# Attention with a depthwise convolution: raw value weights kept apart, three bias rows together, and a later count

## The chip, the cores and the metric

The kernel runs on one core of a Trainium2 chip. A core has five engines with an instruction stream each: TensorE (PE, matrix products; PEld is its loading of the stationary operand), VectorE (DVE), ScalarE (ACT), GpSimd (POOL) and SyncE (SP, which here issues most of the DMAs). Matrix products read SBUF and write to PSUM, the accumulator memory[...]. The metric is the device time in microseconds (us) of one execution; less is better.

## The reference

Four images of 384 channels and 48 x 48 pixels. The queries get the layer-normalized result of a 7 x 7 depthwise convolution added.

```python
x_flat = x.reshape(B, C, N).transpose(0, 2, 1)
local = depthwise_conv_7x7(x, conv_w)          # then batch norm with given statistics
x_norm = _layernorm(x_flat, ln_gamma, ln_beta)
qkv = x_norm @ qkv_w.T + qkv_b
q, k, v = qkv[0], qkv[1], qkv[2]               # 8 heads of 48
q = q + _layernorm(local_flat, ln_gamma, ln_beta)
attn = softmax(q @ k.T * scale)
out = (attn @ v) @ proj_w.T + proj_b
out = x_flat + out
```

All is float32. `ln_gamma` is folded into the weights (each weight row times `gain`), and `ln_beta` into biases: `beta` times the raw weights gives one row of 384 numbers each for queries (0), keys (1) and values (2).

## The kernel before

A tile is eight image rows, that is 384 pixels, of all channels in three chunks of 128; an image has six such groups, and there are 24 tiles. Keys and values of an image stay in SBUF; the tiles of queries then pass one after the other.

The order of the work is written out by hand for TensorE, VectorE and ScalarE: each takes its instructions in the order in which the program text emits them. SP and POOL follow the same rule for the first loads.

**Loads.** The first group of x, then the slab for its convolution, then the three weight blocks of `qkv_wT` (values, keys, queries), then the groups 1 to 5 of x, then `w_o`. Values go straight into `w_v`; keys and queries into `staged[1]` and `staged[0]`, which lie in buffers that later hold keys.

**The start.** `warm` runs filler matmuls. `Norm` holds the steps of a layer norm: mean (L386 for a sum over one chunk, `mean_of` by L473), `centre` (L401), `squares` (L364), `root` (L406 to L408 on ScalarE), `newton` (L413, L414) and `scale` (L468). The convolution is a stream of VectorE operations, one for each tap and chunk, 147 a tile (L251 for the first tap of a chunk, L255 for the others); `convolve_first(n)` takes the next n. For the first tile, ten taps of chunk 0 are made on TensorE instead, by diagonal matrices (`make_diagonals` L263 on ScalarE, `first_products` L274), and added at L827. `AHEAD` is how many taps VectorE does ahead of the first root.

**Biases.** `shift_rows` (L569) multiplies `beta` with the raw weights: values first, in place before `scale_values` (L607) scales them, and keys and queries later. `rows_out` copies the rows to SBUF, `columns` (L596) turns them into columns with 1-row matmuls, and `key_bias`, `query_bias` add them. `scale_rows` (L614, L615) makes the scaled query and key weights.

**The groups of the first image.** `from_x(0, g)` makes three value blocks, three key blocks and three query blocks of group g, two at a time; each pair is one `next` for the products (L473) and one for the ScalarE copies (L506, L512, L525). `both` takes both steps. Between them VectorE normalizes group g + 1, and in the last group the first convolved tile. Pairs use the PSUM buffers of `two_banks`, which alternates between two pools of two buffers.

**The attention.** `attend` makes scores (L767), exponentials on ScalarE (L775) and weighted sums (L788). Twelve slots of two halves make a tile; `plan` shares out the convolution of the coming tiles over the half slots, from the number of taps already done, an estimate of VectorE's spare time (`room`) and the slot by which a tile has to be convolved (`due`). ScalarE's squares for the coming norm (L369) are taken between the exponentials, and wait for VectorE's centring (L445).

**The tail.** Six groups of output projections (L473, L743 adds the residual, L746 sends them out). `divide` gives the reciprocals of the last softmax sums; L1039 multiplies the last outputs by them. `judge[0]` (L1059, L1061) counts sums outside a safe range, `judge[1]` makes a flag of the count, `judge[2]` reads it to decide on a second pass, which does not run here.

Of the kernel before, what the change touches and what calls it, by code (L numbers as in the profile page):

```python
# [10 lines left out]
F32 = mybir.dt.float32  # L11
# [4 lines left out]
P = 128  # L16
# [10 lines left out]
X_LATER = 3  # L27
OUT_SLOT = 4
LAG = 2
AHEAD = 9  # L30
WARM = 12
PE_TAPS = 10

# [5 lines left out]
def segments(a: bass.AP):  # L39

    heads = a[0:288].rearrange("(c h d) f -> h d c f", c=3, h=2)
    tails = a[288:384].rearrange("(h c r) f -> h r c f", h=2, c=3)
    return [(0, heads[0]), (48, tails[0]), (64, heads[1]), (112, tails[1])]
# [3 lines left out]
def unshifted_pass(  # L47
# [16 lines left out]
    nc = tc.nc  # L64
    B, C, N = x.shape
    W = 48
    H = N // W
    CC = C // P
    G = RG * W
    NG = N // G  # L70
# [5 lines left out]
    NT = B * NG  # L76
# [3 lines left out]
    big = ctx.enter_context(tc.tile_pool(name="big", bufs=1))  # L80
    work = ctx.enter_context(tc.tile_pool(name="work", bufs=2))
# [15 lines left out]
    def two_banks():  # L97
        return next(either)()
# [38 lines left out]
    cw, shift, gain, beta = vec[:, :, 0:T0], vec[:, :, T0], vec[:, :, T0 + 1], vec[:, :, T0 + 2]  # L137
# [31 lines left out]
    for c in range(CC):  # L169
        for r, n, first in ((0, HD, 0), (64, HD, 1), (48, 16, 6), (112, 16, 7)):  # L170
            head = first + 2 * c if first < 6 else first
            ch = head * HD + (16 * c if first >= 6 else 0)
            while n:
# [5 lines left out]
                r, n, ch = r + part, n - part, ch + part  # L179
# [4 lines left out]
    w_v = const.tile([P, CC, C], F32, tag="w_v", name="w_v")  # L184
# [2 lines left out]
        work.tile([P, 2, C], F32, tag="pt", name="pt", bufs=5) for _ in range(-(-PE_TAPS // 6))  # L187
    ]
    staged = [
        big.tile([P, CC, C], F32, tag=f"k{NG - 1 - i}", name=f"staged{i}") for i in range(2)  # L190
    ]
    load_packed(w_v, qkv_wT[:, 2 * C :])
    load_packed(staged[1], qkv_wT[:, C : 2 * C])
    load_packed(staged[0], qkv_wT[:, 0:C])
    for g in range(1, NG):
# [1 line left out]
    with nc.allow_non_contiguous_dma(reason="a few vectors, once"):  # L197
        for j in range(2):
            r = 64 * j
# [30 lines left out]
    def conv_ops(t):  # L230
# [10 lines left out]
        if t == 0:  # L241
            mine = [(tap, 0) for tap in taps[PE_TAPS:]]
            order = mine[:AHEAD] + [o for o in order if o[1]] + mine[AHEAD:]
        for tap, c in order:
# [23 lines left out]
    def first_products(n):  # L268

        slab, first, end = slabs[0, 0]  # L270
        for _ in range(n):
            i, tap = coming_products.popleft()
            src, part = window(slab, first_sum, 0, first, end, 0, tap)
            nc.tensor.matmul(  # L274
                part, lhsT=diagonal(i), rhs=src, start=i == 0, stop=i == PE_TAPS - 1
            )
# [45 lines left out]
    each = CC * KS * KS  # L322
# [226 lines left out]
    def both(making):  # L549
        next(making)  # L550
        next(making)
# [3 lines left out]

    row = work.tile([P, CC, G], F32, tag="rb", name="row", bufs=1)

    def of_row(i):  # L560
        return slice(64, 65) if i == 1 else slice(0, 1)

    rows = {}

    def shift_rows(some):
        r = two_banks()
        for c in range(CC):
            for i in some:
                nc.tensor.matmul(  # L569
                    r[of_row(i), i % 2, :C],  # L570
                    lhsT=beta[:, c : c + 1],
                    rhs=staged[i][:, c, :] if i < 2 else w_v[:, c, :],
                    start=c == 0,
                    stop=c == CC - 1,
                )
        rows.update((i, r[of_row(i), i % 2, :C]) for i in some)

    def rows_out(some):
        for i in some:
            dst = row[of_row(i), i].rearrange("o (u h d) -> o u h d", u=CC, h=2)  # L580
            nc.scalar.copy(
                dst[:, :, :, 0:HD], rows[i][:, 0:288].rearrange("o (u h d) -> o u h d", h=2, d=HD)
            )
            nc.scalar.copy(
                dst[:, :, :, HD:64],
                rows[i][:, 288:384].rearrange("o (h u r) -> o u h r", h=2, r=16),
            )

    def columns():

        r = two_banks()
        m = {}
        for i in range(CC):
            m[i] = r[:, i % 2, CC * i : CC * i + CC]
            for c in range(CC):
                nc.tensor.matmul(  # L596
                    m[i][:, c : c + 1],
                    lhsT=row[of_row(i), i, c * P : (c + 1) * P],
                    rhs=one[of_row(i)],
                    start=True,  # L600
                    stop=True,
                )
        return m

    def scale_values():
        for c in range(CC):
            nc.scalar.mul(w_v[:, c], w_v[:, c], gain[:, c : c + 1])  # L607

    def scale_rows(i, c):
        heads = staged[i][:, c, 0:288].rearrange("p (u h d) -> p u h d", h=2, d=HD)  # L610
        tails = staged[i][:, c, 288:384].rearrange("p (h u r) -> p h u r", h=2, r=16)
        for h in range(2):
            w = w_qk[:, c, i, :, 64 * h : 64 * h + 64]
            nc.scalar.mul(w[:, :, 0:HD], heads[:, :, h, :], gain[:, c : c + 1])  # L614
            nc.scalar.mul(w[:, :, HD:64], tails[:, h, :, :], gain[:, c : c + 1])  # L615

    def key_bias(m):
        nc.vector.tensor_add(qkb[:, 1, :], qk_vec[:, 1, :], m[1])
        nc.vector.tensor_add(vbp[:, :, 0], vbp[:, :, 0], m[2])

    def query_bias(m):

        nc.vector.tensor_add(qkb[:, 0, :], qk_vec[:, 0, :], m[0])
        nc.vector.tensor_add(qkb[:, 0, :], qkb[:, 0, :], beta)
# [192 lines left out]
    n_first = 0  # L817

    def convolve_first(n):
        nonlocal n_first  # L820
        n_first += n
        for _ in range(n):
            next(stream)

    def add_products():
        a = accs[0][:, 0, :]
        nc.vector.scalar_tensor_tensor(a, first_sum, shift[:, 0:1], a, ALU.add, ALU.add)  # L827
# [7 lines left out]
    norm = Norm(xn[0, 0])  # L835
# [4 lines left out]
    make_diagonals(0, 5)  # L840
    convolve_first(AHEAD)
    norm.mean_of(norm.buf)
    norm.root()
    make_diagonals(5, PE_TAPS)
    first_products(2)
    shift_rows((2,))
    scale_values()
    first_products(2)
    norm.scale(norm.newton())
    for c in range(CC):  # L850
        scale_rows(1, c)
    for g in range(NG):

        last = g == NG - 1
        making = from_x(0, g)
        both(making)
        if g == 0:
            first_products(PE_TAPS - 4)
        convolve_first(3 if g else 8)
        norm = Norm(accs[0] if last else xn[0, g + 1])  # L860
        norm.sum()
        norm.mean()
        if g == 0:
            shift_rows((1, 0))
            rows_out((2, 1, 0))
        convolve_first(6)
        norm.centre()
        norm.squares()
        next(making)
        if g == 0:  # L870
            add_products()
            m = columns()
            key_bias(m)
            query_bias(m)
        next(making)
        if g == 0:
            for c in range(CC):
                scale_rows(0, c)
        convolve_first(3)
        norm.sum_squares()  # L880
        norm.mean()
        norm.root()
        both(making)
        convolve_first(8 if last else 12)
        if last:
            local_end(0, norm.newton())
        else:
            norm.scale(norm.newton())
        both(making)
        both(making)  # L890
# [3 lines left out]
    for t in range(NT):  # L894
        b, g = divmod(t, NG)
        if g == 0 and b:
# [6 lines left out]
            for gk in range(NG):  # L903
                before = t - NG + gk
                load_residual(before)
                making = from_x(b, gk, before, ao if gk < NG - 1 else outputs[before][0])
# [12 lines left out]
                if gk == 1:  # L919
                    query_end(t)  # L920
                    rb = divide(t - 1)
# [25 lines left out]
        for s in range(NSLOT):  # L947
# [4 lines left out]
            if s == 2 and g:  # L952
                rb = divide(t - 1)
# [57 lines left out]
            if following and s == first - 1:  # L1011
                norm = Norm(accs[t + 1])
# [10 lines left out]
    pair_add()  # L1023
    for before in range(NT - NG, NT):
        ao = aos[before % NG]
        if before == NT - NG + 1:
            judge[0](two_banks()[:, 0, :])
        r, r2 = two_banks(), two_banks()
        parts = r[:, 0, :G], r[:, 1, :G], r2[:, 0, :G]
        for co, m in enumerate(parts):  # L1030
            project(m, lambda c: w_o[:, c, co * P : (co + 1) * P], lambda c: ao[:, c, :])
        for co, m in enumerate(parts):
            finish(before, co, m, nc.scalar)
        if before == NT - NG:
            rb = divide(NT - 1)
        if before == NT - NG + 1:
            judge[1]()
        if before == NT - NG + 2:
            nc.vector.tensor_mul(outputs[NT - 1][0], outputs[NT - 1][0], rb)  # L1039
        if before == NT - 2:  # L1040
            n_outside = judge[2]()
# [536 lines left out]
```

## Time and profile before

| what | value |
|---|---|
| median of three runs | 2867.02 us (2865.14 to 2868.14) |
| profiled execution: device time, span | 2866.66 us, 2864.8 us |
| TensorE busy | 2841.4 us, 99% |
| VectorE busy | 2341.4 us, 82% |
| ScalarE busy | 1650.2 us, 58% |
| mean granted TensorE clock | 0.997 |
| first score (L767) | at 150.94 us |
| last projection (L473) starts | at 2856.93 us |

The page sums up one execution. A line of groups gives the source line, engine, operation, tiles and shapes, then busy time and the mean of one; what stands after it in brackets or behind a bar is the idle time of the engine just before and the instruction that ended it. Matrix products in float32 are two instructions each in the trace, so a projection of three chunks is x6. A busy TensorE is not the same as a fast one: the granted clock is read from the stretches.

### The profile page before, as it was taken

Reading aid. Unit: us, or ns where it says so; the run is one execution under the profiler, and the core shown is the slowest. Engines: PE = TensorE matmul, PEld = TensorE weight load, DVE = VectorE, ACT = ScalarE, POOL = GpSimd, SP = SyncE. Lnnn points to the kernel's source line nnn. Section 1 sums busy time; section 2 is a strip of 40 time slices with the busy share of each in tenths; the row PEclk is TensorE's granted clock in tenths of the full one; section 3 lists DMA queues with packets and bytes.
Section 4 is the critical chain, followed back from the end, with each engine's and each line's share of the span. In section 5 each row is a group of like instructions: output and inputs, shape, how many; then the busy total and the mean of one; then the engine's idle time right before and its main releaser. Section 6 shows DMA issues by size and latency. Waiting matters only on the chain.

```text
span 2864.8 us, 70286 instructions
## 1 busy us (share of the span) xinstructions
PE 2841.4 (99%) x29540; PEld 1463.1 (51%) x29540; DVE 2341.4 (82%) x4613; ACT 1650.2 (58%) x2341; POOL 17.3 (1%) x82
## 2 busy tenths in 40 slices
PE   8999999999999999999999999999999999999998
PEld 5544455444554455555555445545555545555554
DVE  6999999999888988878888889887788887787301
ACT  4356666666226666666622666666652466666662
POOL 2000000000000000000000000000000000000000
PEclk9999999999999999999999999999999999999999
DMA  6101121111220211121132112102113111111111
GB/s 115 39 5 37 44 50 35 30 32 43 72 80 25 48 35 41 31 38 24 38 94 70 28 30 51 35 22 45 38 32 93 45 21 28 43 31 32 46 29 63
DMA packets 103688, 124.38 MB, mean 43 GB/s; under 512 B 43344, under 2 KB 89024, under 8 KB 103360
## 3 DMA queue, kind: packets, MB, share of 16 engines
q1 hardware_dynamic: 99568, 116.07, 17.0%
q8 instruction: 234, 3.83, 0.6%
q10 hardware_dynamic: 3088, 3.65, 0.4%
q14 instruction: 94, 0.77, 0.1%
q0 software_dynamic: 704, 0.06, 0.0%
HBM read 81.98 MB, written 27.03 MB: 38 GB/s over the span
## 4 chain that ended last, share of the span: by engine, by line
PE 95%; DVE 4%; DMA 1%; ACT 0%; issue 0%; SPq 0%; ACTq 0%; DVEq 0%
PE r L767 38%; PE o L788 38%; PE o L473 10%; PE r L473 9%; DVE acc L255 3%; ACT pt L775 0%; DMA xn<-in_x_dram 0%; DMA staged<-in_qkv_wT_dram 0%; DVE xn L401 0%; DMA vec<-natural 0%; PE o L386 0%; PE r L386 0%; DVE sq L375 0%; DMA taps_in<-in_conv_w_dram 0%; DVE sq L374 0%
## 5 line engine op out<-in xcount | busy, mean ns | idle before, releaser
L775 ACT ACTIVATE pt<-r 128x768 f32<-128x768 f32 x1728 | 1400.6, 811 | 754.6 <-PE r L767 738.6
L255 DVE SCALAR_TENSOR_TENSOR acc<-slab,vec,acc 128x368 f32<-128x368 f32 (+7 forms) x3447 | 1756.2, 582 | 3.9 <-DMA slab<-in_x_dram 2.7
L788 PE MATMUL o<-pt,v 64*64 64x384 f32 x13824 | 1440.9, 482 | 0.0
L767 PE MATMUL r<-xn,k 48*64 48x384 f32 x10368 | 1083.1, 482 | 4.8 <-ACT pt L775 4.8
L788 PEld LDWEIGHTS o<-pt,v 64*64 64x64 f32 x13824 | 555.9, 132 | 562.6 <-issue 540.3
L767 PEld LDWEIGHTS r<-xn,k 48*64 48x64 f32 x10368 | 418.9, 132 | 427.4 <-issue 370.5
L767 PE MATMUL r<-qt,kt 48*64 48x384 f32 x3456 | 358.8, 482 | 0.1
L767 PEld LDWEIGHTS r<-qt,kt 48*64 48x64 f32 x3456 | 135.6, 132 | 144.4 <-issue 134.6
L683 DVE TENSOR_TENSOR ao<-o,ao 113x384 f32<-113x384 f32 x72 | 39.9, 554 | 192.8 <-PE r L767 175.7
L473 PE MATMUL o<-xn,w_qk 128*128 128x384 f32 x438 | 149.3, 486 | 0.0
L473 PE MATMUL r<-xn,w_qk 128*128 128x384 f32 x426 | 147.2, 492 | 0.0
L473 PEld LDWEIGHTS o<-xn,w_qk 128*128 128x128 f32 x438 | 83.2, 190 | 58.0
L473 PEld LDWEIGHTS r<-xn,w_qk 128*128 128x128 f32 x426 | 82.1, 193 | 57.9 <-issue 2.7
L506 ACT COPY v<-r 128x384 f32<-128x384 f32 x44 | 19.0, 482 | 130.6 <-PE r L473 130.6
L473 PE MATMUL r<-w_v,xn 128*128 128x384 f32 x264 | 89.3, 487 | 1.2 <-DVE xn L468 1.2
L473 PE MATMUL o<-af,w_o 128*128 128x384 f32 x234 | 80.5, 495 | 0.0
L683 DVE TENSOR_TENSOR aot<-o,aot 113x384 f32<-113x384 f32 x24 | 13.3, 555 | 82.1 <-ACT aot L674 64.6
L374 DVE TENSOR_TENSOR sq<-sq 128x384 f32<-128x384 f32 x47 | 26.0, 554 | 56.2 <-ACT sq L369 56.2
L473 PEld LDWEIGHTS r<-w_v,xn 128*128 128x128 f32 x264 | 49.8, 190 | 37.5 <-issue 3.6
L473 PEld LDWEIGHTS o<-af,w_o 128*128 128x128 f32 x234 | 45.2, 193 | 31.7 <-issue 1.7
L473 PE MATMUL o<-w_v,xn 128*128 128x384 f32 x168 | 58.4, 487 | 0.1
L743 DVE SCALAR_TENSOR_TENSOR xr<-r,pb,xr 128x384 f32<-128x384 f32 x25 | 15.4, 618 | 48.6 <-ACT xn L525 41.7
(130 smaller groups left out, 1026.8 us busy)
## 6 DMA issues: line engine op xcount, KB each, us to landing
xr<-in_x_dram SPq DMA_DIRECT2D x24, 576.0 KB
slab<-in_x_dram SPq DMA_DIRECT2D x32, 378.0 KB
held<-ao SPq DMA_DIRECT2D x20, 576.0 KB
af<-held SPq DMA_DIRECT2D x20, 576.0 KB
xn<-in_x_dram SPq DMA_DIRECT2D x48, 216.0 KB
rb<-rden SPq DMA_DIRECT2D x48, 216.0 KB
out_dram<-xr SPq DMA_DIRECT2D x54, 192.0 KB
slab<-in_x_dram SPq DMA_DIRECT2D x16, 297.0 KB
```

The costliest lines, as they stand in the source:

```text
L255: nc.vector.scalar_tensor_tensor(dst, src, weight, dst, ALU.mult, ALU.add)
L374: nc.vector.tensor_add(self.buf[:, 0, :], src[:, 0, :], src[:, 1, :])
L473: nc.tensor.matmul(dst, lhsT=weights(c), rhs=src(c), start=c == 0, stop=c == CC - 1)
L506: nc.scalar.copy(v[:, blk, :, 0:HD], r[:, :C].rearrange("p (h d) -> p h d", d=HD))
L683: nc.vector.tensor_add(dst, sums[0 : 64 + HA, 1, :G], dst)
L743: nc.vector.scalar_tensor_tensor(xr[:, co, :], m, pb[:, co : co + 1], xr[:, co, :], ALU.add, ALU.add)
L767: nc.tensor.matmul(r[h, j, :G], lhsT=kk[:, blk * P + h.start : blk * P + h.stop], rhs=qq, start=True, stop=True,)
L775: nc.scalar.activation(pt, r[:, :, :G], AF.Exp, scale=SCALE)
L788: nc.tensor.matmul(sums[halves[j], i, :G], lhsT=values[t // NG, kb // NB][h, first : first + 64], rhs=pt[h, j, :], start=kb == 0, stop=kb ...
```

## The change

1. `AHEAD`: 9 taps ahead of the first root become 4.
2. The raw value weights are loaded into a third `staged` tile. `scale_values` reads it and writes `w_v`; it comes right behind the first root on ScalarE, ahead of the second half of the diagonals.
3. Of the ten products, five come before the first norm's scaling and five behind the rows (before: two, two, and six behind the first values).
4. All three rows are made at once behind the first two value blocks, at output partitions 0, 32 and 64 of one bank; `row` is one row long, and the columns use three banks in place of two.
5. Group 0 is written out apart: 14 taps behind the first values, the biases ahead of the third value and first key block (which come before centring), the query weights scaled behind the second root.
6. Groups 1 to 5 take 4 taps ahead of the sum in place of 3.
7. `judge[0]` and `judge[1]` move from the second to the fourth group of the tail.

```diff
-AHEAD = 9
+AHEAD = 4
...
-        big.tile([P, CC, C], F32, tag=f"k{NG - 1 - i}", name=f"staged{i}") for i in range(2)
+        big.tile([P, CC, C], F32, tag=f"k{NG - 1 - i}", name=f"staged{i}") for i in range(3)
...
-    load_packed(w_v, qkv_wT[:, 2 * C :])
+    load_packed(staged[2], qkv_wT[:, 2 * C :])
...
-    row = work.tile([P, CC, G], F32, tag="rb", name="row", bufs=1)
+    row = work.tile([P, CC, G], F32, tag="rb", name="row", bufs=1)[:, 0]
...
     def of_row(i):
-        return slice(64, 65) if i == 1 else slice(0, 1)
+        return slice(32 * i, 32 * i + 1)
...
         for c in range(CC):
-            for i in some:
+            for i in range(3):
                 nc.tensor.matmul(
-                    r[of_row(i), i % 2, :C],
+                    r[of_row(i), 0, :C],
                     lhsT=beta[:, c : c + 1],
-                    rhs=staged[i][:, c, :] if i < 2 else w_v[:, c, :],
+                    rhs=staged[i][:, c, :],
...
-        r = two_banks()
-        m = {}
-        for i in range(CC):
-            m[i] = r[:, i % 2, CC * i : CC * i + CC]
+        r, r2 = two_banks(), two_banks()
+        m = {1: r[:, 0, 0:CC], 2: r[:, 1, 0:CC], 0: r2[:, 0, 0:CC]}
+        for i in m:
...
-            nc.scalar.mul(w_v[:, c], w_v[:, c], gain[:, c : c + 1])
+            nc.scalar.mul(w_v[:, c], staged[2][:, c], gain[:, c : c + 1])
...
     norm.root()
+    scale_values()
+    first_products(5)
+    norm.scale(norm.newton())
     make_diagonals(5, PE_TAPS)
-    first_products(2)
-    shift_rows((2,))
-    scale_values()
-    first_products(2)
-    norm.scale(norm.newton())
     for c in range(CC):
         scale_rows(1, c)
-    for g in range(NG):
+
+    making = from_x(0, 0)
+    both(making)
+    shift_rows()
+    rows_out()
+    first_products(PE_TAPS - 5)
+    m = columns()
+    convolve_first(14)
+    norm = Norm(xn[0, 1])
+    norm.sum()
+    norm.mean()
+    add_products()
+    key_bias(m)
+    query_bias(m)
+    both(making)
+    convolve_first(3)
+    norm.centre()
+    norm.squares()
+    convolve_first(4)
+    norm.sum_squares()
+    norm.mean()
+    norm.root()
+    for c in range(CC):
+        scale_rows(0, c)
+    both(making)
+    convolve_first(10)
+    norm.scale(norm.newton())
+    both(making)
+    both(making)
+    for g in range(1, NG):
...
-        convolve_first(3 if g else 8)
+        convolve_first(4)
...
-        if before == NT - NG + 1:
+        if before == NT - NG + 3:
             judge[0](two_banks()[:, 0, :])
...
-        if before == NT - NG + 1:
+        if before == NT - NG + 3:
             judge[1]()
```

More of the change, by code (lines that the diff above doesn't have):

```diff
@@ L554, in unshifted_pass, with shift_rows @@
     qkb = const.tile([P, 2, CC], F32, tag="qkb", name="qkb")
-    row = work.tile([P, CC, G], F32, tag="rb", name="row", bufs=1)
+    row = work.tile([P, CC, G], F32, tag="rb", name="row", bufs=1)[:, 0]
+    rows = {}
     def of_row(i):
-        return slice(64, 65) if i == 1 else slice(0, 1)
-    rows = {}
-    def shift_rows(some):
+        return slice(32 * i, 32 * i + 1)
+    def shift_rows():
         r = two_banks()
         for c in range(CC):
-            for i in some:
+            for i in range(3):
                 nc.tensor.matmul(
-                    r[of_row(i), i % 2, :C],
+                    r[of_row(i), 0, :C],
                     lhsT=beta[:, c : c + 1],
-                    rhs=staged[i][:, c, :] if i < 2 else w_v[:, c, :],
+                    rhs=staged[i][:, c, :],
                     start=c == 0,
@@ L575, in shift_rows, with rows_out @@
                 )
[L576 to L580, printed above, removed]
+        rows.update((i, r[of_row(i), 0, :C]) for i in range(3))
+    def rows_out():
+        for i in (1, 2, 0):
+            dst = row[of_row(i)].rearrange("o (u h d) -> o u h d", u=CC, h=2)
             nc.scalar.copy(
@@ L597, in columns @@
                     m[i][:, c : c + 1],
-                    lhsT=row[of_row(i), i, c * P : (c + 1) * P],
+                    lhsT=row[of_row(i), c * P : (c + 1) * P],
                     rhs=one[of_row(i)],
@@ L856, in unshifted_pass @@
         both(making)
-        if g == 0:
-            first_products(PE_TAPS - 4)
-        convolve_first(3 if g else 8)
+        convolve_first(4)
+        assert not last or n_first >= each - PE_TAPS
         norm = Norm(accs[0] if last else xn[0, g + 1])
@@ L862, in unshifted_pass @@
         norm.mean()
-        if g == 0:
-            shift_rows((1, 0))
-            rows_out((2, 1, 0))
         convolve_first(6)
@@ L868, in unshifted_pass @@
         norm.squares()
[L869 to L878, printed above, removed]
+        both(making)
         convolve_first(3)
```

## The prediction

> **What bounds the kernel now.** First the page's busy shares and its chain of waits:
>
> ```profile
> PE 2841.4 (99%) x29540; PEld 1463.1 (51%) x29540; DVE 2341.4 (82%) x4613; ACT 1650.2 (58%) x2341; POOL 17.3 (1%) x82
> ...
> PE 95%; DVE 4%; DMA 1%; ACT 0%; issue 0%; SPq 0%; ACTq 0%; DVEq 0%
> ```
>
> TensorE sets the end, so only its idle time, its slow stretches, or work taken off it can be won. Next, who TensorE waited for over the whole span:
>
> ```profile
> PE r L767 <- ACT pt L775: 4.8, 8, 2.8
> PE o L386 <- DVE sq L375: 4.1, 2, 3.8
> PE r L1061 <- DVE outside L1059: 2.9, 1, 2.9
> PE o L832 <- POOL one L151: 1.9, 1, 1.9
> PE o L569 <- DMA w_v<-in_qkv_wT_dram: 1.8, 1, 1.8
> PE r L473 <- DVE xn L468: 1.2, 1, 1.2
> ```
>
> (columns: us in total, times, longest us.) Three places matter: the start (L386, L569, L473), one stall of 2.8 us among the scores (L767), and the count of the tail (L1061). The chain as a timeline of the start ends with these pieces:
>
> ```profile
> 41.01 0.57 DVE sq L375
> 41.58 0.14 issue
> 41.71 1.62 PE o L386 x2
> 43.33 6.00 PE r L473 x12
> 49.34 3.87 PE o L473 x12
> ```
>
> Up to 41.71 us TensorE is led by loads, VectorE and ScalarE; from there it is never idle for long until 311 us. Note 6.00 us for twelve matmul instructions that take 3.87 next time: the windows of 2 us show a granted clock of 0.67, 0.50, 0.50 and 0.62 from 40 to 48 us.
>
> **What the Trainium skill says.** (1) "TensorE: Matmul & The Clock Gate", Part 1, What's actually happening: after an idle window of some 3.4 us, in a grid that runs free of the kernel, the TensorE clock is halved until a window has been busy. The trace agrees: half clock after the idle stretch at 38 to 41.7 us and after the one at 2825 to 2828 us; the stall of 2.8 us at 311.9 us brought none, so the placing in the grid counts. (2) The same page, Part 3, Measured speedup vs the span model: three column tiles together give 2.38 times. The trace shows two: L569 with one row (x6) and with two rows (x12) each took 2.10 us. Three are not shown. (3) The same page, Architectural detail, on queues: ScalarE and VectorE take their instructions strictly in order. I use that for what stands behind what. No page gives a time for the loads of this start; the trace does.
>
> **The change, part by part.** I follow the new program order with old durations.
>
> *First root.* VectorE ran nine tap operations ahead of the first Newton step (L413), which had been ready on ScalarE's side much earlier:
>
> ```profile
> 13.81 5.47 DVE L255 SCALAR_TENSOR_TENSOR acc<-slab,vec,acc 128x329 f32<-128x329 f32 x9 [2.73 <-DMA slab<-in_x_dram]
> ...
> 15.41 0.52 ACT L408 ACTIVATE sq<-sq 128x384 f32<-128x384 f32 x1
> ...
> 19.20 0.61 DVE L413 SCALAR_TENSOR_TENSOR sq<-r,eps,sq 128x384 f32<-128x384 f32 x1
> ...
> 20.44 1.36 DVE L468 SCALAR_TENSOR_TENSOR xn<-xn,sq 128x1152 f32<-128x1152 f32 x1
> ...
> 21.94 4.11 PE L473 MATMUL r<-w_v,xn 128*128 128x384 f32 x12 [1.21 <-DVE xn L468]
> ```
>
> Four take 4 x 0.61 = 2.4 us, to 16.25, just past the root's end at 15.93. So the normalized group is there at 18.8 instead of 21.8, and the first values start at about 18.95: **3.0 us earlier**. Value weights: the load landed at 17.17 (L569 waited for it); scaling was in place behind that row, 18.03 to 19.93. Now it reads the raw copy, so starts at 17.2 and ends at 19.1; the third chunk is needed at 20.2, so it costs nothing. The five diagonals behind it (1.55) and the key rows (3.3) end at 23.9 on ScalarE, used only from 28 us. The SP queue issues the same loads in the same order, with another destination.
>
> *The rows.* First values end at 23.0. The three rows then need the query weights. Their landing is not shown; the neighbours landed at 17.17, 20.36 and, after it in the queue, 26.75 (first L374), some 3.2 us apart, so an estimate of 23.5; bounds 20.4 and 30.2, where the old rows ran without waiting. Cost of eighteen instructions: between 2.1 (three tiles together) and 4.2 us (a third alone). I take 2.1, to 25.7. Six ScalarE copies (0.54 per row) end at 27.4, hidden behind five products (10 x 0.32 = 3.2 us) to 28.85. The columns (1.49 as before) end at 30.3: before, 37.95.
>
> *The second normalization.* The 14 taps (7.1 us) end at 26.0, under the wait for the second group's load at 26.75; its sum ends at 28.0. The product addition at 28.9, four bias operations to 31.3, three taps to 32.9 and centring to 34.2. TensorE: mean, then third values and first keys to 34.85. Here order costs something: the squares (L364) now stand behind the ScalarE copies of these two, which wait for 34.85, so squares run 36.0 to 37.2; the four taps fit below. The sum of squares ends at 38.4 and the mean starts at 38.5 instead of 41.71: **3.2 us earlier**, after 3.65 us of idle (3.8 before).
>
> *What follows.* Mean and six key projections take 4.6 us at full clock. Query weights are scaled after the root, to about 45.1 on ScalarE, where they stood ahead of it before; at full clock the queries lose 0.5 to that. The group's last projection would then end at 49.4, against 55.0: 5.6 won. With the half clock as now it is 51.7: 3.3. The idle stretch is longer than the window, so I expect the half clock in most placings: **3.5 us**, ends 1.2 (rows not together) and 5.6.
>
> *Groups 1 to 5.* One more tap (0.55) ahead of each sum. VectorE's idle before L401 was 4.32, 1.77, 2.38, 0.86 and 0.49 us in turn, so it is hidden but for some 0.1 in the last. Total taps before the first scores: 154 becomes 156, that is 17 and 19 of the second tile.
>
> *The stall at 311 us.* VectorE is full from 160 to 313 us, and TensorE waits for it by way of ScalarE:
>
> ```profile
> 313.41 0.52 ACT L369 ACTIVATE sq<-acc 128x384 f32<-128x384 f32 x1 [3.83 <-DVE acc L445]
> ...
> 314.69 0.88 PE L767 MATMUL r<-xn,k 48*64 48x384 f32 x8 [2.80 <-ACT pt L775]
> ```
>
> Working out the planner's shares with 17 and with 19 gives the same running total, 302, at that slot. Two operations fewer are left: 2 x 0.52 = **1.0 us** off the stall (bounds 0 and 1.3).
>
> *The tail.* Now:
>
> ```profile
> 2827.91 0.21 PE L1061 MATMUL r<-outside,ones_col 128*1 128x24 f32 x2 [2.86 <-DVE outside L1059]
> 2828.04 1.26 PEld L473 LDWEIGHTS o<-af,w_o 128*128 128x128 f32 x5
> 2828.04 5.83 PE L473 MATMUL o<-af,w_o 128*128 128x384 f32 x12
> ...
> 2842.19 1.35 DVE L1039 TENSOR_TENSOR ao<-ao,rb 128x1152 f32<-128x1152 f32 x1
> ```
>
> Projections could have gone on at 2824.9: 3.15 us lost, and 1.8 more at half clock (5.83 against 4.03). Moved two groups on, the count is a new wait: it stands on VectorE behind the third addition of the group before (0.66 after the last matmul) and behind L1039 (1.35), then takes 0.18. Behind it on TensorE wait nine projections of the fourth group. Price about 2.6 us, with no gain of its own. The broadcast that L1039 needs was issued by 2830.4 and its traffic is over by about 2834, before 2837.3. The flag is read 5.8 us later; hidden. Net 4.95 - 2.6 = 2.35 at full clock, 0.65 with another half-clock window: **1.5 us**.
>
> Sum: 3.5 + 1.0 + 1.5 = **6.0 us**. The profiled span is 2864.8 (device time 2866.66), the median 2867.02: 2861.0.
>
> **The rivals.** *Full clock*: neither idle stretch falls on the grid: 5.6 + 1.0 + 2.35 = 9.0, so 2858. For it: the stall at 311.9; against it: 3.65 us exceed a window. *Gain mostly eaten*: the third column tile runs alone (2.1 us on TensorE's path) or the half clock lasts two windows: 1.2 + 1.0 + 0.65 = 2.9, so 2864.1. For it: two windows were lost at 40 us; against: two tiles already overlap fully. *Slower*: all three rows now wait for the last weight load, and products, columns and third values stand behind them. If it lands at the upper bound 30.2, TensorE idles 7 us from 23.0, everything behind moves by 6.6 and one half-clock window (1.7) follows: 3.5 - 8.3 + 2.5 = -2.3, so 2869.3, more with two windows. It decides from a landing some 6 us after my 23.5; loads landing 3.2 us apart in queue order speak against it.
>
> **How the numbers follow.** Forecast 0.50, with 2859 to 2863 as its own range; full clock 0.22; mostly eaten 0.20; slower 0.08. A measurement can tell about 0.2%, 5.7 us, so 2861.3 is a bound close to my figure: two thirds of the forecast's own chance lie beyond it (0.33), with full clock 0.55. Slower by that much: 0.06. Same: 0.39. The range 2856.5 to 2866 leaves out the slower case and the ends of the others.
>
> **What would show it.** First values near 19.0 us; L569 as eighteen instructions in 2.1 us near 23.6; L386 near 38.5; the first L767 near 147.5 instead of 150.94; the stall at L767 near 1.8; L1061 after L1039 with 2.5 us of idle. It is wrong if the rows wait past 25 us, if L386 is not earlier, or if a group after the first loses TensorE time to VectorE.

## The result

| | before | changed |
|---|---|---|
| median of 6 runs each, taken together | 2866.32 us (2865.14 to 2868.14) | 2858.84 us (2857.59 to 2860.61) |
| ratio | | 0.9973, 95% interval 0.9961 to 0.9986 |
| span of the profiled execution | 2864.8 us | 2857.1 us |

The change makes the kernel 7.5 us faster. The forecast was 6.0. In a second comparison (12 runs of the changed kernel) it was 2860.38 against 2866.35, that is 6.0 us, 0.9979 (0.9970 to 0.9987). The runs of the changed kernel differ among themselves by some 4 us; the experiments show one source, half clock that falls differently from one execution to the next.

Where the time went is read from fixed points of TensorE's work in the two traces (its timeline, start of an instruction):

| point | before | changed | ahead by |
|---|---|---|---|
| first values (L473) | 21.94 | 19.11 | 2.83 |
| mean of the second sum of squares (L386) | 41.71 | 37.78 | 3.93 |
| first values of group 1 | 54.98 | 49.87 | 5.11 |
| first score | 150.94 | 146.40 | 4.54 |
| end of the stall among the scores | 314.69 | 309.11 | 5.58 |
| first projection of the tail | 2818.97 | 2813.15 | 5.82 |
| last residual addition (VectorE) | 2859.07 | 2850.76 | 8.31 |
| end of the span | 2864.8 | 2857.1 | 7.7 |

So some 4.5 us come from the first image (5.1 from group 0, of which groups 1 to 5 lose 0.6), 1.0 from the stall, 0.2 from the long stretch behind it, and 2.5 from the tail, of which 0.6 are lost again behind the last addition.

The profile after, first who TensorE waited for over the whole span (us in total, times, longest):

```profile
PE o L386 <- DVE sq L375: 3.6, 2, 3.4
PE r L765 <- ACT pt L773: 3.4, 7, 1.8
PE r L1073 <- DVE outside L1071: 2.1, 1, 2.1
PE o L830 <- POOL one L151: 1.9, 1, 1.9
PE o L473 <- DVE xn L468: 1.7, 1, 1.7
PE o L386 <- ACT k L512: 1.1, 1, 1.1
```

The same three places remain: the wait for the second sum of squares (3.4 of it, 3.8 before), the stall of the scores (L765 is the old L767; 1.8, 2.8 before), and the count (L1073, the old L1061; 2.1, 2.9 before). New is the last line: 1.1 us behind a key copy in group 4.

The timeline of the start, with the first root, the first values, the three rows and the second mean:

```profile
14.01 2.44 DVE L255 SCALAR_TENSOR_TENSOR acc<-slab,vec,acc 128x329 f32<-128x329 f32 x4 [2.95 <-DMA slab<-in_x_dram]
...
16.36 0.61 DVE L413 SCALAR_TENSOR_TENSOR sq<-r,eps,sq 128x384 f32<-128x384 f32 x1
...
19.11 4.11 PE L473 MATMUL o<-w_v,xn 128*128 128x384 f32 x12 [1.72 <-DVE xn L468]
...
23.15 2.11 PE L568 MATMUL r<-staged,vec 128*1 128x384 f32 x18
...
34.44 0.48 ACT L506 COPY v<-r 128x384 f32<-128x384 f32 x1 [7.51 <-PE r L473]
34.81 0.59 ACT L512 ACTIVATE k<-r,qkb 128x384 f32<-128x384 f32 x1
35.29 1.16 ACT L364 ACTIVATE sq<-xn 128x1152 f32<-128x1152 f32 x1
...
37.78 0.88 PE L386 MATMUL o<-sq,mean_w 128*128 128x384 f32 x2 [3.38 <-DVE sq L375]
...
38.50 5.73 PE L473 MATMUL r<-xn,w_qk 128*128 128x384 f32 x12
```

All eighteen instructions of the rows (L568) take 2.11 us, as six did before. The squares stand on ScalarE behind the copies of the third values and first keys, as forecast; TensorE is idle for 3.38 us, and its next twelve matmul instructions take 5.73 us, not 4.03.

The tail, TensorE's and VectorE's timeline:

```profile
2831.41 1.35 DVE L1051 TENSOR_TENSOR ao<-ao,rb 128x1152 f32<-128x1152 f32 x1
2832.68 0.17 DVE L1071 TENSOR_SCALAR outside<-inside 128x24 f32<-128x24 f32 x1
...
2832.90 0.21 PE L1073 MATMUL r<-outside,ones_col 128*1 128x24 f32 x2 [2.06 <-DVE outside L1071]
...
2833.04 4.14 PE L473 MATMUL o<-af,w_o 128*128 128x384 f32 x12
```

The mark (L1071) waits behind the multiplication L1051, as forecast, and in this execution no half clock follows (4.14 us, 5.83 before).

### The profile page after: what moved, and what is told of

It is laid out like the page before. It is cut to its first block, busy times and chain, and to the rows that moved or that the text cites. A ratio compares the mean times of both kernels' runs of the same rounds, so it can differ in the third digit from the quotient of the medians.

```text
span 2857.1 us, 70279 instructions
## 1 busy us (share of the span) xinstructions
PE 2835.6 (99%) x29540; PEld 1447.8 (51%) x29540; DVE 2341.4 (82%) x4613; ACT 1650.3 (58%) x2341; POOL 17.3 (1%) x82
## 3 DMA queue, kind: packets, MB, share of 16 engines
q10 hardware_dynamic: 3088, 3.65, 0.4%
## 4 chain that ended last, share of the span: by engine, by line
PE 93%; DVE 5%; DMA 0%; ACT 0%; issue 0%; SPq 0%; DVEq 0%; ACTq 0%
PE r L765 37%; PE o L786 37%; PE o L473 10%; PE r L473 10%; DVE acc L255 4%; DMA slab<-in_x_dram 0%; ACT pt L773 0%; PE r L386 0%; PE o L386 0%; DVE sq L375 0%; PE o L274 0%; DVE sq L374 0%; DVE acc L401 0%; DVE xn L401 0%; DVE ao L681 0%
## 5 line engine op out<-in xcount | busy, mean ns | idle before, releaser
L255 DVE SCALAR_TENSOR_TENSOR acc<-slab,vec,acc 128x368 f32<-128x368 f32 (+6 forms) x3447 | 1756.5, 584 | 4.1 <-DMA slab<-in_x_dram 2.9
L765 PE MATMUL r<-xn,k 48*64 48x384 f32 x10368 | 1081.3, 482 | 3.4 <-ACT pt L773 3.4
L786 PEld LDWEIGHTS o<-pt,v 64*64 64x64 f32 x13824 | 549.9, 132 | 568.9 <-issue 541.4
L765 PEld LDWEIGHTS r<-xn,k 48*64 48x64 f32 x10368 | 414.7, 132 | 430.0 <-issue 370.4
L765 PE MATMUL r<-qt,kt 48*64 48x384 f32 x3456 | 357.7, 482 | 0.1
L765 PEld LDWEIGHTS r<-qt,kt 48*64 48x64 f32 x3456 | 133.4, 132 | 146.5 <-issue 135.0
L473 PE MATMUL r<-xn,w_qk 128*128 128x384 f32 x432 | 148.9, 490 | 0.0
L473 PE MATMUL o<-xn,w_qk 128*128 128x384 f32 x432 | 147.2, 486 | 0.0
L473 PEld LDWEIGHTS r<-xn,w_qk 128*128 128x128 f32 x432 | 82.8, 192 | 58.2 <-issue 1.8
L473 PEld LDWEIGHTS o<-xn,w_qk 128*128 128x128 f32 x432 | 82.1, 190 | 57.2
L473 PE MATMUL r<-w_v,xn 128*128 128x384 f32 x258 | 87.3, 487 | 0.0
L473 PE MATMUL o<-af,w_o 128*128 128x384 f32 x222 | 75.0, 486 | 0.0
L473 PEld LDWEIGHTS r<-w_v,xn 128*128 128x128 f32 x258 | 48.8, 190 | 35.2 <-issue 1.8
L473 PE MATMUL o<-w_v,xn 128*128 128x384 f32 x174 | 60.3, 486 | 1.7 <-DVE xn L468 1.7
L473 PEld LDWEIGHTS o<-af,w_o 128*128 128x128 f32 x222 | 42.1, 190 | 29.2
```

The lines of the kernel that those rows point to most:

```text
L255: nc.vector.scalar_tensor_tensor(dst, src, weight, dst, ALU.mult, ALU.add)
L473: nc.tensor.matmul(dst, lhsT=weights(c), rhs=src(c), start=c == 0, stop=c == CC - 1)
L765: nc.tensor.matmul(r[h, j, :G], lhsT=kk[:, blk * P + h.start : blk * P + h.stop], rhs=qq, start=True, stop=True,)
L786: nc.tensor.matmul(sums[halves[j], i, :G], lhsT=values[t // NG, kb // NB][h, first : first + 64], rhs=pt[h, j, :], start=kb == 0, stop=kb ...
```

## The experiments

My theory was the sum of the prediction: three places on TensorE's path, each with a local gain that is kept to the end. The first rival was that VectorE, which is full up to the stall, takes the start's gain back. The second was that the half clock, and with it mostly luck, makes the difference. Each kernel was compared with the kernel before in the same group of runs; "against before" is the difference of these medians. The changed kernel itself stands at 7.5 and 6.0 us faster by this measure. The intervals of most variants overlap with its own, so a difference of some 3 us from the changed kernel is not told by the totals alone; it is read from the traces, one execution of each kernel.

### The count of the tail put back (a1_count_back)

```diff
-        if before == NT - NG + 3:
+        if before == NT - NG + 1:
             judge[0](two_banks()[:, 0, :])
...
-        if before == NT - NG + 3:
+        if before == NT - NG + 1:
             judge[1]()
```

> The changed kernel with the count of the tail back in its second group. Sum of local gains (my theory): TensorE waits about 2.9 us for the mark of the sums again, where it waits 2.06 us now, and a window of half clock may follow (1.8 us); the other half of the change keeps its gain. 1.9 to 2.6 us slower than the changed kernel, about 2861.0. Rival, the tail is set by the sending of the outputs and not by TensorE: under 0.4 us, 2859.

Measured: 2860.38 against 2865.70, 5.3 us faster than before (0.9982, 0.9975 to 0.9989), so 0.7 to 2.2 us less than the changed kernel. In the trace TensorE waits 2.78 us again, and the following twelve instructions take 5.83 us; from the tail's first projection to the last addition it is 40.01 us, where the changed kernel needs 37.61. The span ends 5.1 us behind that addition, against 5.7. The traces show the direction; the totals, whose intervals overlap, show neither it nor a size of 2 us.

### The late count alone (c3_before_late_count)

The same edit the other way round, on the kernel before.

> The kernel before with the count of the tail in the fourth group and nothing else of the change. If the tail's gain stands by itself: TensorE waits 2.1 us for the mark behind L1039's multiplication in place of 2.86 us with 1.8 us of half clock behind it, its last product comes 2.5 us earlier against the start of the tail, and the whole is 1.9 to 2.5 us faster than before, 2863.7. Rival: under 0.5 us, 2865.5.

Measured: 2866.20 against 2866.35, ratio 0.9996 (0.9988 to 1.0005): no gain that can be told. The timeline of this kernel's TensorE shows why:

```profile
2838.61 0.21 PE L1061 MATMUL r<-outside,ones_col 128*1 128x24 f32 x2 [2.06 <-DVE outside L1059]
2838.75 5.83 PE L473 MATMUL o<-af,w_o 128*128 128x384 f32 x12
```

The wait is the shorter one, but half clock follows it here too (5.83 us). What is left, 0.8 us from the tail's first projection to the last addition, goes behind the last addition (5.9 us to the end of the span in place of 5.1). Between this run and the changed kernel, the late count is worth 0.8 to 2.5 us of TensorE's time, by where half clock falls, and less of the total.

All traces with the count in these two places, from the tail's first projection to the end of the span:

| count | behind it | kernels | us |
|---|---|---|---|
| second group | half clock | before, a1, c4 | 45.7 to 46.5 |
| fourth group | half clock | a3, c2, c3 | 45.8 to 46.0 |
| fourth group | full clock | changed, c1, a2, a4, b1, b2 | 44.0 to 44.3 |

So up to the end of the span the later count gained some 1.8 us in the executions in which half clock stayed away, and nothing in those in which it came.

### Four taps ahead of the root alone (c4_before_four_ahead)

```diff
-AHEAD = 9
+AHEAD = 4
...
-        convolve_first(3 if g else 8)
+        convolve_first(3 if g else 13)
```

> The kernel before with four tap operations ahead of the first root, and thirteen in place of eight behind it, and nothing else of the change. The first values should start near 19.0 in place of 21.94. Theory: that alone is not kept, since the second normalization waits for the second group's load (26.8 us) and stands behind six more taps, so its mean stays near 41.7: under 0.5 us, 2865.5. Rival, the earlier root is worth its 2.9 us by itself: 2863.

Measured: 2865.30 against 2866.35, ratio 0.9997 (0.9989 to 1.0005). The first values start at 20.14 us, 1.8 earlier, since products and the value row still stand ahead of them. But of that nothing is kept. The timeline of this kernel:

```profile
20.14 4.03 PE L473 MATMUL r<-w_v,xn 128*128 128x384 f32 x12
...
26.80 0.56 DVE L374 TENSOR_TENSOR sq<-xn 128x384 f32<-128x384 f32 x1 [1.22 <-DMA xn<-in_x_dram]
...
30.86 1.35 DVE L401 TENSOR_TENSOR xn<-xn,o 128x1152 f32<-128x1152 f32 x1
...
41.52 1.62 PE L386 MATMUL o<-sq,mean_w 128*128 128x384 f32 x2 [3.69 <-DVE sq L375]
```

VectorE has the same number of taps ahead of the second group's sum, five of them now behind the root, and waits there for the load as it did in the kernel before, whose line is:

```profile
26.87 0.56 DVE L374 TENSOR_TENSOR sq<-xn 128x384 f32<-128x384 f32 x1 [1.19 <-DMA xn<-in_x_dram]
```

The load ends the wait at 26.80 in place of 26.87, and the second mean is at 41.52, in place of 41.71. The early root pays only with the new order behind it: rows, products and bias columns are through at 29.45 us, not 37.95.

### Nine taps ahead of the root, in the new order (a2_nine_ahead)

```diff
-AHEAD = 4
+AHEAD = 9
...
-    convolve_first(14)
+    convolve_first(9)
```

> The changed kernel with nine tap operations ahead of the first root in place of four, and nine in place of fourteen behind it, so that their number before the scores stays. My theory: first values start near 21.9 us in place of 19.11, and all behind them on TensorE moves with them: 2.5 to 3.0 us slower than the changed kernel, 2861.5. Rival, VectorE decides anyway because it is full in the scores up to 309 us, and what TensorE gains at the start is given back there: under 0.5 us, and the stall of the scores near 309 us shorter than 1.76 us by what is lost at the start.

Measured: 2864.24 against 2865.70, only 1.5 us faster than before (0.9994, 0.9986 to 1.0002). This is a larger loss than either theory gave. TensorE waits 4.7 us for the first group, and then half clock covers the values. Its timeline, then its stretches (us, busy times of five engines, clock, DMA share, GB/s):

```profile
22.45 6.77 PE L473 MATMUL o<-w_v,xn 128*128 128x384 f32 x12 [4.75 <-DVE xn L468]
```

```profile
22.00:24.00 2.00, 1.55 (x3) 0.97 (x4) 2.00 (x5) 2.00 (x8) 0.00 (x0) 0.50 1.11 185
24.00:26.00 2.00, 2.00 (x5) 1.09 (x4) 2.00 (x5) 0.03 (x1) 0.00 (x0) 0.50 1.08 173
```

3.3 us are the later root and 2.7 the slower values, 6.0 at the start of group 1. The first score is at 151.84, 5.44 us later than in the changed kernel, and the stall ends 5.46 us later: between these two points VectorE gives nothing back and takes nothing. That speaks against the first rival. Groups 1 to 5 do give 0.56 us back, since `AHEAD` also sets the order of the taps; the account of the prediction takes this up.

### The same with TensorE kept busy (b1_nine_filled)

```diff
     first_products(5)
+    filler = two_banks()[:, 0, 0:P]
+    for _ in range(18):
+        nc.tensor.matmul(filler, lhsT=mean_w, rhs=ident, start=True, stop=True)
+    two_banks()
     norm.scale(norm.newton())
```

> a2_nine_ahead with eighteen filler matmuls (some 4.3 us) on TensorE in its wait of 4.7 us for the first normalized group. The run of a2 lost 3.3 us by the later root and 2.7 us more by half clock over the first values. If the second part comes from TensorE's idle time alone, the values take 4.1 us again and 2.7 us are won back: 2861.5, and what stays against the changed kernel (about 2.8 us) is the root itself. If the half clock comes from the phase of a grid that the fillers can't move, or the fillers get in the way: 2864, as a2.

Measured: 2862.44 against 2865.86, 3.4 us faster than before (0.9987, 0.9980 to 0.9993). The stretch from 24 us on, again as the view of stretches:

```profile
24.00:26.00 2.00, 2.00 (x9) 0.86 (x10) 2.00 (x5) 0.09 (x1) 0.00 (x0) 1.00 1.07 245
```

The values start at 21.77 and take 4.11 us; the first score is at 148.49. So half clock came from TensorE's idle time; it made 2.7 us of the loss of a2 in the trace, and in the totals, against before, 2.0 us came back. What stays, 2.66 us at the start of group 1 and 2.09 at the first score, is the later root; against before it is 2.6 to 4.1 us less gain. In other words the five products moved ahead of the first values need the early root: with nine taps they leave a hole that costs the clock.

### Two column tiles in place of three (a3_two_tiles)

```diff
-        return slice(32 * i, 32 * i + 1)
+        return slice(64, 65) if i == 1 else slice(0, 1)
...
-                    r[of_row(i), 0, :C],
+                    r[of_row(i), i // 2, :C],
```

with `row` again of three rows.

> The changed kernel with value and query rows in the same column tile (partition 0, two banks) and only the key row apart. My theory: the eighteen instructions of the rows take 4.2 us in place of 2.11, and the bias columns, the second mean and all behind them come 2.1 us later: 2860.9. Rival, it is hidden since the second normalization waits for ScalarE's copies and squares: the rows take 4.2 us, the total moves by under 0.5 us.

Measured: 2862.43 against 2865.70, 3.3 us faster than before (0.9988, 0.9980 to 0.9997), so 2.7 to 4.2 less than the changed kernel. The timeline of TensorE:

```profile
23.61 4.03 PE L568 MATMUL r<-staged,vec 128*1 128x384 f32 x18
```

The rows take 4.03 us in place of 2.11, and the first score comes at 149.16, 2.76 later: 1.92 by the rows, 0.46 by a later start of this execution (values at 19.47), and 0.4 by the bias columns, which with two row positions take 1.7 us to the next instruction in place of 1.3. Half clock behind the second mean cost 1.7 us here as in the changed kernel. The rows are on the path, not hidden; the part of the total above the forecast has half clock in the tail beside it (5.74 us behind the count in this execution).

### The squares first (a4_squares_first)

```diff
-    both(making)
+    next(making)
     convolve_first(3)
     norm.centre()
     norm.squares()
+    next(making)
     convolve_first(4)
```

> The changed kernel with the squares of the second normalization ahead of the ScalarE copies of the third value and first key block. They then run near 32.9 us in place of 35.29, the second sum is there near 36.0 in place of 37.65, so the mean near 36.1: 1.7 us earlier. If the half clock from 38.5 us on follows from the idle stretch ahead of it, the shorter stretch (1.7 us) brings none and 1.7 us more are won: 2855.4. If the half clock comes from something else (the narrow products of the columns): 2857.1.

Measured: 2856.97 against 2865.70, 8.7 us faster than before (0.9969, 0.9958 to 0.9980), 1.2 to 2.7 better than the changed kernel. The timeline:

```profile
33.46 1.16 ACT L364 ACTIVATE sq<-xn 128x1152 f32<-128x1152 f32 x1 [5.95 <-DVE xn L401]
35.03 0.48 ACT L506 COPY v<-r 128x384 f32<-128x384 f32 x1 [0.41 <-PE r L473]
...
36.58 0.88 PE L386 MATMUL o<-sq,mean_w 128*128 128x384 f32 x2 [1.58 <-DVE sq L375]
37.30 4.03 PE L473 MATMUL r<-xn,w_qk 128*128 128x384 f32 x12
```

The squares no longer wait for the products; the mean is 1.2 us earlier, TensorE idles 1.58 us, the key products run at full clock, and the first score is at 143.57, 2.83 us earlier than in the changed kernel. The order that the change chose for ScalarE costs this much: 1.2 us, and the half clock. Of the nine traces with 3.38 us of idle ahead of this mean eight have half clock behind it (b2 is the ninth), of the two with 1.58 us (a4 and b4) none. The total did not quite reach the 2855.4 us expected for that case.

### Taps moved to where VectorE waits (b2_taps_moved)

```diff
-        convolve_first(4)
+        convolve_first(3)
...
-        convolve_first(6)
+        convolve_first(9 if g < 4 else 6)
         norm.centre()
```

> The changed kernel with three taps (not four) ahead of the sum in groups 1 to 5, and nine in place of six ahead of the centring in groups 1 to 3, where VectorE still waits 1.5 to 3.6 us for the mean. 23 in place of 19 operations of the second tile are done ahead of the scores. My theory: TensorE's wait of 1.06 us in group 4 (L386 behind ScalarE's key copy) goes, 0.75 us of it on the path, and the stall near 309 us shrinks from 1.76 by 4 x 0.52 us, so to nothing: 2.5 us faster than the changed kernel, 2856.3. Rival, the stall is not VectorE's lateness but the order on ScalarE: 0.75 us, 2858.1, with the stall as it was.

Measured: 2856.94 against 2865.86, 8.9 us faster than before (0.9970, 0.9958 to 0.9982). Half of the expectation failed: groups 1 to 5 win only 0.23 us (first score less start of group 1's values: 96.30, in the changed kernel 96.53), since small waits appear in other groups. And the stall did not vanish:

```profile
306.22 1.51 PE L765 MATMUL r<-xn,k 48*64 48x384 f32 x8 [1.91 <-ACT pt L773]
```

But the time from the first score to the end of the stall went from 162.71 to 161.17 us, 1.54 us for four operations where 2.08 were expected. The stall alone is a poor measure, as the next two runs show. Part of this kernel's shorter span (2854.7 us, 2.4 below the changed kernel's) is not due to the edit: its execution had no half clock in group 0, and 1.12 us of it stand already at the start of group 1 (48.75 against 49.87).

### The changed kernel again, and two taps less (c1_changed_again, c2_two_taps_less)

```diff
     both(making)
-    convolve_first(10)
+    convolve_first(8)
     norm.scale(norm.newton())
```

> The changed kernel once more, beside the others of this group: 2858.8, within 1 us. The stall of the scores near 309 us should be 1.8 us where half clock comes after the narrow products near 175 us, and some 3.2 us where it doesn't (as in three other runs), and from the first score to the end of the stall 162.7 to 163.1 us either way, if VectorE sets that end.

> The changed kernel with two tap operations less in group 0 (eight in place of ten behind the second sum of squares), so 17 of the second tile ahead of the scores, as in the kernel before. If VectorE's count of operations sets the end of the stall: from the first score to the end of the stall 163.75 us as before (162.71 in the changed kernel), the first score itself where it is, and 1.0 us slower than the changed kernel, 2859.9. If not: 2858.8 with the stall unmoved.

Measured: 2860.38 and 2860.96 against 2866.35 (0.9979, 0.9970 to 0.9987, and 0.9980, 0.9972 to 0.9988); the totals cannot tell the two apart, and c1 itself misses its expectation (2858.8 within 1 us). The traces can tell them. From the first score to the end of the stall:

| taps of the second tile done ahead | kernels | us |
|---|---|---|
| 17 | before, c2, c3, c4 | 163.75, 163.75, 163.75, 163.74 |
| 19 | changed, c1, a1, a2, a3, a4, b1, b3 | 162.71, 162.70, 163.06, 162.73, 163.00, 162.72, 162.71, 162.72 |
| 23 | b2, b4 | 161.17, 161.17 |

Two taps are 1.04 us, as forecast. In a1, a3 and b3 the stall itself is 3.0 to 3.3 us, and its end is within 0.4 us of where it was. Those are executions (b2 and b4 too) without half clock behind the narrow products of L473 (18 instructions, one column each) near 175 us. The view of stretches of the changed kernel, then of a1:

```profile
174.00:176.00 2.00, 2.00 (x22) 1.46 (x26) 1.22 (x5) 0.16 (x1) 0.00 (x0) 0.88 0.02 4
176.00:178.00 2.00, 2.00 (x20) 0.87 (x16) 2.00 (x5) 0.81 (x1) 0.00 (x0) 0.50 0.03 10
```

```profile
174.00:176.00 2.00, 2.00 (x26) 1.30 (x29) 1.22 (x5) 0.63 (x2) 0.00 (x0) 1.00 0.03 8
176.00:178.00 2.00, 2.00 (x32) 0.94 (x28) 2.00 (x5) 1.16 (x2) 0.00 (x0) 1.00 0.00 2
```

and a1's stall, in TensorE's timeline:

```profile
308.95 0.88 PE L765 MATMUL r<-xn,k 48*64 48x384 f32 x8 [3.34 <-ACT pt L773]
```

Where TensorE is faster, it waits longer: VectorE's number of operations sets this end, and half clock ahead of it costs nothing.

c1 and b2 also show what differs from run to run. Both have the same idle stretch ahead of the second mean. TensorE's timeline of c1, then of b2:

```profile
38.04 1.62 PE L386 MATMUL o<-sq,mean_w 128*128 128x384 f32 x2 [3.38 <-DVE sq L375]
39.45 6.17 PE L473 MATMUL r<-xn,w_qk 128*128 128x384 f32 x12
```

```profile
38.28 0.88 PE L386 MATMUL o<-sq,mean_w 128*128 128x384 f32 x2 [3.38 <-DVE sq L375]
39.00 4.03 PE L473 MATMUL r<-xn,w_qk 128*128 128x384 f32 x12
```

3.38 us of idle cost 2.9 us in one (0.74 and 2.14), nothing in the other, and 1.7 in the first profile of the changed kernel. So the length of the stretch alone does not decide. That fits what the Trainium skill says in "TensorE: Matmul & The Clock Gate", Part 1, of a window that runs free of the kernel.

### The mark early (b3_mark_early), and three edits together (b4_all_three)

```diff
-        if before == NT - NG + 3:
+        if before == NT - NG + 2:
             judge[0](two_banks()[:, 0, :])
...
             rb = divide(NT - 1)
+            judge[3]()
...
-        def count(m):
+        def mark():
             nc.vector.tensor_scalar(outside, inside, 0.5, None, ALU.is_lt)
+
+        def count(m):
```

with the flag also made in the third group.

> The changed kernel with the mark of the sums on VectorE right behind the reciprocals in the first group of the tail, and only the count's matmul later, in the third group. TensorE should wait for nothing in the tail: 2.06 us of idle and some 0.3 us of restart go, so 2.3 us faster than the changed kernel, 2856.5. Rival, the end is set by the outputs' sending or the flag: TensorE ends 2.3 us earlier and the span by under 1 us, 2858.

> a4_squares_first, b2_taps_moved and b3_mark_early in one kernel. If the three gains lie in three places of TensorE's path, they add up: 2.3 + 2.5 + 2.3 = 7.1 us against the changed kernel, 2851.7. If VectorE's fullness in the first scores takes back what group 0 gains: 2854.

Measured: b3 2857.80, b4 2852.12, both against 2865.86: 8.1 us (0.9970, 0.9958 to 0.9982) and 13.7 us (0.9951, 0.9937 to 0.9964) faster than before. In b3 TensorE waits for nothing in the tail, and from its first projection to the last addition it is 35.47 us in place of 37.61; of these 2.14 us some 0.4 go behind the last addition (6.1 in place of 5.7). So the span is shorter with TensorE's end, as the theory has it; the total lies near the rival's 2858 and cannot decide. The waits of b4's TensorE over the whole span:

```profile
PE r L765 <- ACT pt L773: 3.7, 7, 1.9
PE o L830 <- POOL one L151: 1.9, 1, 1.9
PE o L473 <- DVE xn L468: 1.6, 1, 1.6
PE o L386 <- DVE sq L375: 1.6, 1, 1.6
```

Its span is 2849.8 us, 7.3 below the changed kernel's, where the sum of the three was to be 7.1. Place by place it has what each edit gave alone: the second mean at 36.22 (a4: 36.58), 161.17 us from the first score to the end of the stall (b2: 161.17), 35.47 in the tail (b3: 35.47). The gains lie in three places and add up. Of all the kernels here it is the fastest.

## Why the prediction was right

**The first root.** Forecast 18.95 us for the first values, measured 19.11. The step was right, but c4 shows that by itself it is worth nothing that can be told (0.9997, 0.9989 to 1.0005), and a2 with b1 that within the new order it is worth 2.7 us at the start of group 1 (2.1 at the first score), and more than twice as much with the half clock that its absence brings. The prediction did follow the whole new order, and that is what made the sum come out; had it stopped at "3.0 us earlier" it would have been right by chance.

**The rows.** Three tiles together: 2.11 us (forecast 2.1), on the path (a3). The weights' load was never waited for beyond 0.4 us; the slower rival rested on that and falls. The columns ended at 29.45, forecast 30.3: in three row positions they took 1.1 us in place of 1.49.

**The second normalization.** Mean at 37.78, forecast 38.5; the idle stretch 3.38, forecast 3.65; the squares behind ScalarE's copies, as forecast, and a4 shows that this order costs 1.2 us and often the clock. Group 0 gained 5.11 us at the start of group 1, forecast 3.3 to 5.6, as one window of half clock, some 3.4 us, came in this profile (two in c1, none in b2). The 3.5 us taken for it was too low for this execution; with c1's 51.26 us the gain is 3.7. Half clock behind the mean cost c1 as much as the kernel before (2.9 us each), so these 3.7 us are the order's own and no luck of the clock. The 0.5 us set aside for the late query weights did not come: in b2, at full clock, group 1 starts 10.47 us after the mean, where the forecast has 10.9.

**Groups 1 to 5.** This step failed. "Hidden but for some 0.1 in the last" was 0.57 us lost, of it most in group 4, where TensorE waits 1.06 us. The twelve taps of group 3 on VectorE show it, before and changed:

```profile
101.74 5.75 DVE L255 SCALAR_TENSOR_TENSOR acc<-slab,vec,acc 128x368 f32<-128x368 f32 x12
```

```profile
96.47 6.83 DVE L255 SCALAR_TENSOR_TENSOR acc<-slab,vec,acc 128x360 f32<-128x360 f32 x12
```

The first tile's stream takes `AHEAD` taps of chunk 0, then chunks 1 and 2, then the rest of chunk 0. With four ahead in place of nine it comes back to chunk 0 five operations sooner, and the first it meets there are large ones. a2 and b1 show that this is the cause, and not the one more tap: they have the same four taps ahead of each sum but the old order, their twelve take 5.75 us again, and from group 1 to the first score they need 95.97 and 95.96 us, as the kernel before (95.96; changed 96.53). So the added tap was hidden, and the early root cost 0.57 us here. The forecast took one more tap at a mean price and did not see that the others change too. One of its own signs of being wrong, a later group that loses TensorE time to VectorE, came true here; the size, 0.57 us of some 7, leaves the sum standing.

**The stall.** Forecast 1.8 us, measured 1.76, and the count of taps behind it is shown by c2.

**The tail.** Forecast wait 2.5 us, measured 2.06; forecast gain 1.5, between 0.65 and 2.35 by the clock. TensorE's part gained 2.49 in the changed kernel and 0.8 in c3, so these ends were right. That a part of it does not reach the end of the span was not foreseen: there it is 1.9 in the changed kernel and nothing in c3. That the 1.5 taken for it lies close to the first of these is in part luck.

The rival that VectorE takes the start back up to the stall is false (a2: 5.44 us at the first score, 5.46 at the stall's end); all that it took are the 0.57 us of groups 1 to 5. The rival of full clock is half true: it came in the tail of the first profile and not in group 0, and by c1, c2 and c3 it is a matter of the single execution. The prediction saw the idle window of some 3.4 us, which it has from the Trainium skill, borne out by the trace, but the stretch of 2.86 us that it names for the tail is shorter than that window already, and half clock followed 2.06 us in three traces. Here the measurement decides: a wholly idle window of that length is not needed.

## What to carry to other kernels

An engine's earlier start is worth what the next wait on its path leaves of it: follow the new order to the point where both traces run in step, and cost what stands behind each moved instruction on its engine. On TensorE price an idle stretch twice, once for itself and once for half clock behind it, and keep the second as a range. Where another engine's count of operations sets an end (here VectorE's, at the stall), take operations off that engine; a faster TensorE only waits longer. And where operations come from one ordered stream, a number changed in one place changes which operations stand in every later place: price those anew.

## What the runs showed of the hardware

- Three column tiles of one column each, over 384 elements, ran as fast as one: x18 in 2.11 us, x6 in 2.10. The Trainium skill's "TensorE: Matmul & The Clock Gate", Part 3, Measured speedup vs the span model, has 2.38 times; here it is three times, and the measurement decides. Two tiles of which one is used twice took 4.03.
- Half clock followed idle stretches of 2.06 us (a3, c2, c3; not in six other traces with the same stretch) and 2.78 (a1), and not one of 3.38 (b2); it followed the narrow products near 175 us, where TensorE counts as busy, in nine of the fourteen profiles (not in a1, a3, b2, b3 and b4).
- From the last addition to the end of the span it is 5.1 us in two kernels (before, a1) and 5.6 to 6.2 in the others. What sets it stays open; no run varied it alone. The place of the count is not enough to explain it, as c4 has the early count of these two and 5.7 us.
